# Top-p by a 27-step bit descent, and GAT weights factored into per-node exponentials, on one Trainium2 core

## The chip, the cores and the metric

The kernel runs on one core of a Trainium2 chip. The metric is the device time of one execution in microseconds (us); lower is better. A core has TensorE (PE, matrix products), VectorE (DVE), ScalarE (ACT, table functions and copies), GpSimd (POOL) and SyncE (SP, which issues most transfers).

## The reference

The input is `x`, 3327 nodes by 256 features, and `adj`, a dense 3327 x 3327 array with about 0.5% non-zero entries. Two graph layers follow one another, each added to its input, each behind a layer norm and a ReLU.

```
# layer 0, two steps
q = X @ W1.T @ W2.T;  k = X @ W3.T
probs = softmax(q @ k.T)                    # 3327 x 3327
idx = argsort(-probs);  sp = probs sorted;  cs = cumsum(sp)
keep_sorted = cs - sp < 0.9                 # top-p: largest entries up to 90% of the mass
A = probs * mask;  A = A / A.sum(-1)
Xf = R @ Xf;  Xa = A @ Xa                   # R: adj + identity, rows scaled to sum 1
Z += Xf @ U1[n].T + Xa @ U2[n].T

# layer 1, 4 heads of 64
hp = h @ W;  s = hp . a_src;  d = hp . a_dst          # per node and head
e = leaky_relu(s[i] + d[j], 0.2), -inf where adj[i, j] <= 0
out = elu(softmax(e) @ hp)
```

## The kernel before

Rows are cut into 26 tiles of 128 (`NT`), the last padded by one row. The program has two functions. `fast` computes everything and leaves a flag, `redo`; `general` is an older program for the same result, which runs only when the flag is set, behind a runtime branch in `tile_gnn`. The order of instructions on each engine is not written out by hand: a scheduler takes the operations in program order as their priority and lets later ones go ahead where earlier ones are not ready. [...]

**Layer 0.** `main`, `xf1` and `xa1` hold the features of all nodes with a column of ones. In each of the two steps, a first loop projects all tiles to `kt` (keys, transposed) and adds up a Gram matrix `gm`. Then 13 groups of two tiles follow. For a group:
- `exponentials` computes the queries, the logits against all keys in seven matrix products (L602), and their exponentials `e`, 128 x 3327 (L603). It also takes the mean and the variance of the logits from `gm`.
- `full_step` multiplies a tile of the adjacency with the features (L739) and scales the rows.
- `top_p` finds, for each row, the threshold under which the small entries sum to a tenth of the row. A guess comes from the moments of the logits by a polynomial (`QUANTILE`). `below` (L658) adds up the entries under a threshold in one pass of DVE over 3327 numbers. Three passes (first step) or four (second step) with secant updates bring the threshold near, a last pass and a search for maxima (L701 and on) pick the exact cut from a window of 32 values, and L728 sets the entries under it to zero.
- `attention_step` transposes `e` in blocks (L755), copies them out of PSUM (L757) and multiplies them with the features (L764).
- In the second step `add_up` applies `U1` and `U2` and prepares the layer norm.

The exponentials of the next group stand ahead of this group's `top_p` in the program. `epool` has four buffers for `e`, so two groups are in flight.

**Layer 1.** After the layer norm, each tile is projected to `hp` (four heads of 64 and a column of ones), and the scores `sd` are multiplied and reduced on DVE (L885, L886). The destination scores are spread over all partitions in `db`. A stage then reads the adjacency row by row (`an`), turns it into a mask of large negative numbers (L902), and takes for each row and head the largest masked score (L905). This gives the row maxima of the softmax, so that `pq` holds two terms per row: `s - top` and `0.2 s - top`.

The last loop goes over blocks of four row tiles, and in each over all 26 column tiles j. `broadcasts` spreads the row terms over partitions (`both`). Per j and head, the logit is the larger of two sums: ACT adds one (L954), DVE the other and takes the maximum (L955). Then DVE caps it at zero (L959), ACT takes the exponential (L960), DVE multiplies with the adjacency's sign (L963), and PE adds `hp` times the weights to one accumulator per head (L964). Column 65 of each accumulator holds the denominators. At the end of a block the accumulators are copied, transposed, divided, passed through ELU and stored.

Last, `redo` is made from marks in `met` that the top-p search left.

Of the kernel before, what the change touches and what calls it, by code (L numbers as in the profile page):

```python
# [24 lines left out]
H = 4  # L25
# [15 lines left out]

EVALS = (3, 4)
AIM = 13.0
WIN = 32
PIECES = 16
PIECE = 208
NC = 7
QUANTILE = (0.0080475, 0.1178442, 0.6505088, 2.0535298, 1.2031906)
# [416 lines left out]

@with_exitstack
def fast(
# [31 lines left out]
    met = const.tile([P, 5, STEPS * NT], F32, name="met")  # L499

# [12 lines left out]
    with ExitStack() as l0:  # L513
# [11 lines left out]
        gm = wpool.tile([DA, 2 * DA + 1], F32, name="gm")  # L525
        V.tensor_copy(gm[:, :DA], ident[:DA, :DA])
# [3 lines left out]
        scr = l0.enter_context(tc.tile_pool(name="scr", bufs=1))  # L530
# [41 lines left out]
        def exponentials(src, tiles):  # L572


            G = len(tiles)
            sm = small.tile([P, G], F32, name="sm")
            mu = small.tile([P, G], F32, name="mu")
            sq = small.tile([P, G], F32, name="sq")
            es = []
            for g, t in enumerate(tiles):  # L580
                ps = projected(w1, transposed(src, t))
                ut = small.tile([DA, P], F32, name="ut")
                S.copy(ut, ps)
                ps = ps_m.tile([DA, P], F32, name="pm")
                T.matmul(ps, w2, ut, start=True, stop=True)
                qt = small.tile([DA, P], F32, name="qt")
                S.copy(qt, ps)
                ps = ps_m.tile([P, 2 * DA + 1], F32, name="pm")
                T.matmul(ps, qt, gm, start=True, stop=True)
                qg = small.tile([P, 2 * DA + 1], F32, name="qg")  # L590
                S.copy(qg, ps)
                V.tensor_copy(mu[:, g : g + 1], qg[:, 2 * DA :])
                V.scalar_tensor_tensor(
                    qg[:, :DA], qg[:, :DA], 1.0, qg[:, DA : 2 * DA], ALU.mult, ALU.mult, accum_out=sq[:, g : g + 1]
                )
                e = epool.tile([P, NP], F32, name="e")
                nc.gpsimd.memset(e[:, N:], 0.0)
                parts = small.tile([P, NC], F32, name="parts")
                for c in range(NC):
                    w = min(512, N - 512 * c)  # L600
                    pl = ps_l.tile([P, 512], F32, name="pl")
                    T.matmul(pl[:, :w], qt, kt[:, 512 * c : 512 * c + w], start=True, stop=True)  # L602
                    S.activation(  # L603
                        e[:, 512 * c : 512 * c + w], pl[:, :w], AF.Exp, accum_out=parts[:, c : c + 1]
                    )
                V.tensor_reduce(sm[:, g : g + 1], parts, AX.X, ALU.add)
                es.append(e)
            return es, sm, mu, sq

        def top_p(es, sm, mu, sq, n, tiles):  # L610
# [3 lines left out]

            G, i0 = len(es), n * NT + tiles[0]

            def small_tile(name):
                return small.tile([P, G], F32, name=name)

            b = small_tile("b")  # L620
            V.tensor_scalar(b, sm, 1.0 - TOP_P, None, ALU.mult)
            V.tensor_copy(met[:, 0, i0 : i0 + G], sm)
            var = small_tile("var")
            V.tensor_mul(var, mu, mu)
            V.tensor_sub(var, sq, var)
            V.tensor_scalar(var, var, 1e-6, None, ALU.max)
            sg = small_tile("sg")
            S.activation(sg, var, AF.Ln)
            S.activation(sg, sg, AF.Exp, scale=0.5)
            u = small_tile("u")  # L630
            S.activation(u, b, AF.Ln, scale=1.0 / N)
            V.tensor_sub(u, u, mu)
            V.scalar_tensor_tensor(u, var, -0.5, u, ALU.mult, ALU.add)
            V.tensor_scalar(u, u, -6.0, -0.3, ALU.max, ALU.min)
            w = small_tile("w")
            V.tensor_scalar(w, u, QUANTILE[0], None, ALU.mult)
            for c in QUANTILE[1:-1]:
                V.scalar_tensor_tensor(w, w, c, u, ALU.add, ALU.mult)
            V.scalar_tensor_tensor(w, w, QUANTILE[-1], sg, ALU.add, ALU.add)
            t = small_tile("t0")  # L640
            V.tensor_mul(t, w, sg)
            V.tensor_add(t, t, mu)
            S.activation(t, t, AF.Exp)
            g = small_tile("g0")
            V.tensor_mul(g, w, w)
            S.activation(g, g, AF.Exp, scale=0.5)
            V.scalar_tensor_tensor(g, g, math.sqrt(2 * math.pi) / N, sg, ALU.mult, ALU.mult)
            V.tensor_scalar(g, g, 0.25, None, ALU.min)

            k2 = small_tile("k2")  # L650
            V.scalar_tensor_tensor(k2, t, 225.0, t, ALU.mult, ALU.mult)

            def below(th, outs=None, dst=None):
                sums = small_tile("sums") if dst is None else dst
                ys = []
                for k, e in enumerate(es):
                    y = scr.tile([P, N], F32, name="y", bufs=1)
                    V.scalar_tensor_tensor(  # L658
                        y, e[:, :N], th[:, k : k + 1], e[:, :N], ALU.is_lt, ALU.mult, accum_out=sums[:, k : k + 1]
                    )  # L660
                    if outs is not None:
                        outs(k, y)
                return sums

            tp = bp = None
            for k in range(EVALS[n]):
                B = below(t)
                if k > 0:
                    dt, dB, kg = small_tile("dt"), small_tile("dB"), small_tile("kg")
                    V.tensor_sub(dt, t, tp)  # L670
                    V.tensor_sub(dB, B, bp)
                    V.tensor_mul(dt, dt, dB)
                    V.tensor_mul(dB, dB, dB)
                    V.tensor_add(dB, dB, k2)
                    V.tensor_mul(kg, k2, g)
                    V.tensor_add(dt, dt, kg)
                    V.reciprocal(dB, dB)
                    V.tensor_mul(g, dt, dB)
                x, d, nt = small_tile("x"), small_tile("d"), small_tile("nt")
                V.tensor_scalar(x, g, AIM / 2, 1.0, ALU.mult, ALU.add)  # L680
                V.reciprocal(x, x)
                V.scalar_tensor_tensor(x, x, AIM, t, ALU.mult, ALU.mult)
                V.tensor_sub(d, b, B)
                V.tensor_add(d, d, x)
                V.tensor_mul(d, d, g)
                V.tensor_add(d, d, t)
                V.scalar_tensor_tensor(d, t, 0.25, d, ALU.mult, ALU.max)
                V.scalar_tensor_tensor(nt, t, 8.0, d, ALU.mult, ALU.min)
                tp, bp, t = t, B, nt

            up = small_tile("up")
            V.tensor_sub(up, sm, b)
            V.scalar_tensor_tensor(up, t, 16.0, up, ALU.mult, ALU.is_ge)
            V.scalar_tensor_tensor(up, up, BIG, t, ALU.mult, ALU.max)

            cands = small.tile([P, G, PIECES, 8], F32, name="cands")
            wins = small.tile([P, G, WIN], F32, name="wins")

            def window(k, y):
                for c in range(PIECES):  # L700
                    V.max(cands[:, k, c, :], y[:, c * PIECE : min(c * PIECE + PIECE, N)])  # L701

            B = below(up, window)
            V.tensor_reduce(met[:, 1, i0 : i0 + G], cands[:, :, :, 7], AX.X, ALU.max)
            room = small_tile("room")
            V.tensor_sub(room, B, b)
            for k, e in enumerate(es):
                flat = cands[:, k].rearrange("p c r -> p (c r)")
                for r in range(WIN // 8):
                    top = wins[:, k, 8 * r : 8 * r + 8]  # L710
                    V.max(top, flat)
                    if r < WIN // 8 - 1:
                        V.match_replace(flat, top, flat, -1.0)
                win = wins[:, k, :]
                cum = small.tile([P, WIN], F32, name="cum")
                V.tensor_tensor_scan(cum, win, win, 0.0, ALU.add, ALU.bypass)
                keep = small.tile([P, WIN], F32, name="keep")
                V.scalar_tensor_tensor(
                    keep, cum, room[:, k : k + 1], win, ALU.subtract, ALU.is_lt,
                    accum_out=met[:, 2, i0 + k : i0 + k + 1],  # L720
# [339 lines left out]
```

## Time and profile before

| | |
|---|---|
| median of 3 runs | 4061.26 us (4054.56 to 4062.52) |
| profiled execution | 4062.52 us, span 4060.7 us |
| mean granted TensorE clock | 0.855 of full |
| layer 0, from the span's start to the last `top_p` | 0 to 2308 us |
| last attention and sums of layer 0 | 2308 to 2362 us |
| layer norm and projection of layer 1 | 2362 to 2480 us |
| row maxima (L902, L905) | 2480 to 2930 us |
| loop over blocks, and the end | 2930 to 4061 us |

Times in the profile are from the first instruction of the span. A row of a group gives the source line, the engine, the operation, the tiles that it writes and reads with their sizes, the number of instructions, the busy time in us, the mean of one in ns, and then the engine's idle time just before such instructions with what ended it. PEclk is the granted clock of TensorE in tenths, in 40 equal slices of the span. In the timeline the columns are start and duration in us, engine, line, operation and tiles; start to start is the pitch, and durations of neighbours overlap a little.

### The profile page before, as it was taken

Reading aid. Unit: us, or ns where it says so; the run is one execution under the profiler, and the core shown is the slowest. Engines: PE = TensorE matmul, PEld = TensorE weight load, DVE = VectorE, ACT = ScalarE, POOL = GpSimd, SP = SyncE. Lnnn points to the kernel's source line nnn. Section 1 sums busy time; section 2 is a strip of 40 time slices with the busy share of each in tenths; the row PEclk is TensorE's granted clock in tenths of the full one; section 3 lists DMA queues with packets and bytes.
Section 4 is the critical chain, followed back from the end, with each engine's and each line's share of the span. In section 5 each row is a group of like instructions: output and inputs, shape, how many; then the busy total and the mean of one; then the engine's idle time right before and its main releaser. Section 6 shows DMA issues by size and latency. Waiting matters only on the chain.

```text
span 4060.7 us, 34714 instructions
## 1 busy us (share of the span) xinstructions
PE 2928.3 (72%) x11286; PEld 1822.5 (45%) x11286; DVE 3364.6 (83%) x7077; ACT 1616.4 (40%) x2997; POOL 56.7 (1%) x167
## 2 busy tenths in 40 slices
PE   6689999999994999999999942000076667666665
PEld 4366676676861776677766831000022122121122
DVE  2498788788607998788887779999499999999998
ACT  3423333333232333323333222000177777777765
POOL 0000000000000000000000020000000000000000
PEclk9589999899995999999999966555589899998888
DMA  3011111111210111111111121232111111111110
GB/s 99 0 34 34 51 51 34 47 55 34 68 34 0 37 38 38 39 60 45 38 38 37 54 75 67 102 116 101 37 42 42 45 44 44 44 47 42 47 34 25
DMA packets 80959, 195.13 MB, mean 48 GB/s; under 512 B 5890, under 2 KB 64001, under 8 KB 77441
## 3 DMA queue, kind: packets, MB, share of 16 engines
q1 hardware_dynamic: 78384, 190.83, 14.6%
q10 hardware_dynamic: 2384, 1.98, 0.2%
q8 instruction: 91, 1.49, 0.2%
q14 instruction: 100, 0.82, 0.1%
HBM read 189.39 MB, written 3.41 MB: 47 GB/s over the span
## 4 chain that ended last, share of the span: by engine, by line
DVE 61%; PE 26%; ACT 6%; issue 4%; another core or an unknown queue 1%; DMA 1%; POOL 1%; ACTq 0%; DVEq 0%; POOLq 0%; SPq 0%
DVE y L658 16%; DVE e L955 10%; DVE junk L905 9%; PE pl L602 8%; DVE e L963 8%; PE acc L739 6%; DVE e L959 4%; DVE cands L701 4%; PE acc L764 2%; PE pm L789 1%; PE pm L569 1%; DVE an L902 1%; PE acc L964 1%; ACT e L603 1%
## 5 line engine op out<-in xcount | busy, mean ns | idle before, releaser
L964 PE MATMUL acc<-e,hp 128*65 128x512 f32 (+1 forms) x1456 | 721.5, 644 | 344.1 <-DVE e L963 344.1
L964 PEld LDWEIGHTS acc<-e,hp 128*65 128x65 f32 x1456 | 209.0, 155 | 831.4 <-DVE e L963 587.6
L757 ACT COPY et<-pt 128x512 f32<-128x512 f32 (+1 forms) x364 | 199.5, 555 | 747.2 <-PE pt L755 747.2
L658 DVE SCALAR_TENSOR_TENSOR y<-e,nt 128x3327 f32<-128x3327 f32 x130 | 478.8, 3683 | 2.3
L955 DVE SCALAR_TENSOR_TENSOR e<-both,sd,e 128x512 f32<-128x512 f32 (+1 forms) x728 | 472.4, 712 | 8.7 <-ACT e L954 8.7
L954 ACT ACTIVATE e<-both,dlow 128x512 f32<-128x512 f32 (+1 forms) x728 | 443.8, 678 | 52.6 <-PE acc L964 52.6
L602 PE MATMUL pl<-kt,qt 64*128 64x512 f32 (+1 forms) x728 | 411.4, 705 | 53.5 <-ACT e L603 53.5
L963 DVE SCALAR_TENSOR_TENSOR e<-adjb,e 128x512 f32<-128x512 f32 (+1 forms) x728 | 428.2, 652 | 4.4 <-ACT e L960 4.2
L960 ACT ACTIVATE e<-e 128x2048 f32<-128x2048 f32 (+1 forms) x182 | 325.3, 1787 | 244.3 <-DVE e L959 244.2
L905 DVE CUSTOM_DVE_ANT_0 junk<-an,db 128x3327 bf16<-128x3327 f32 (+1 forms) x104 | 370.7, 3624 | 2.0 <-ACT db L890 1.2
L935 PE MATMUL pb<-ident,pq 128*128 128x128 f32 x208 | 32.1, 301 | 469.6 <-DVE pq L914 466.3
L739 PE MATMUL acc<-main,at 128*128 128x257 f32 x1352 | 336.6, 402 | 0.8 <-DMA at<-in_adjt_dram 0.8
L739 PE MATMUL acc<-xf,at 128*128 128x257 f32 x1352 | 336.5, 398 | 0.3 <-ACT xa L768 0.3
L764 PE MATMUL acc<-xa,et 128*128 128x257 f32 x1352 | 322.3, 382 | 3.8 <-ACT et L757 3.8
L764 PE MATMUL acc<-main,et 128*128 128x257 f32 x1352 | 324.3, 384 | 0.2
L739 PEld LDWEIGHTS acc<-main,at 128*128 128x128 f32 x1352 | 263.3, 201 | 52.4 <-issue 13.1
L739 PEld LDWEIGHTS acc<-xf,at 128*128 128x128 f32 x1352 | 257.5, 198 | 49.1 <-issue 14.0
L602 PEld LDWEIGHTS pl<-kt,qt 64*128 64x128 f32 x728 | 146.3, 225 | 292.7 <-ACT e L603 227.9
L755 PE MATMUL pt<-ident,e 128*128 128x128 f32 x1352 | 202.2, 275 | 94.0 <-DVE e L728 94.0
L603 ACT ACTIVATE e<-pl 128x512 f32<-128x512 f32 (+1 forms) x364 | 205.2, 564 | 158.4 <-PE pl L602 155.4
L764 PEld LDWEIGHTS acc<-main,et 128*128 128x128 f32 x1352 | 246.0, 191 | 35.3 <-ACT et L757 6.2
L764 PEld LDWEIGHTS acc<-xa,et 128*128 128x128 f32 x1352 | 245.4, 191 | 36.4 <-ACT et L757 7.6
(192 smaller groups left out, 3359.0 us busy)
## 6 DMA issues: line engine op xcount, KB each, us to landing
at<-in_adjt_dram SPq DMA_DIRECT2D x104, 832.0 KB, 4.5
an<-in_adj_dram SPq DMA_DIRECT2D x25, 1663.5 KB, 6.9
adjb<-in_adjt_dram SPq DMA_DIRECT2D x78, 512.0 KB, 3.8
main<-in_x_dram SPq DMA_DIRECT2D x26, 128.0 KB, 3.2
xh<-in_x_dram SPq DMA_DIRECT2D x26, 128.0 KB, 2.0
xr<-in_x_dram SPq DMA_DIRECT2D x26, 128.0 KB, 2.0
adjb<-in_adjt_dram SPq DMA_DIRECT2D x13, 256.0 KB, 2.8
out_dram<-r SPq DMA_DIRECT2D x25, 128.0 KB, 1.8
```

The source lines that it names most:

```text
L602: T.matmul(pl[:, :w], qt, kt[:, 512 * c : 512 * c + w], start=True, stop=True)
L603: S.activation(e[:, 512 * c : 512 * c + w], pl[:, :w], AF.Exp, accum_out=parts[:, c : c + 1])
L658: V.scalar_tensor_tensor(y, e[:, :N], th[:, k : k + 1], e[:, :N], ALU.is_lt, ALU.mult, accum_out=sums[:, k : k + 1])
L739: T.matmul(acc, at[:, j - j0, :], src[:, j, :], start=(j == 0), stop=(j == NT - 1))
L755: T.transpose(pt[:, k, :], e[:, (j0 + k) * P : (j0 + k + 1) * P], ident)
L764: T.matmul(acc, et[:, j - j0, :], src[:, j, :], start=(j == 0), stop=(j == NT - 1))
L905: V.tensor_tensor_reduce(junk[:p], an[:p], db[:p, k, :N], scale=1.0, scalar=-BIG, op0=ALU.add, op1=ALU.max, accum_out=top[:p, t, k : k + 1],)
L954: S.activation(e[:, k, :w], both[:, 1, k, :w], AF.Identity, bias=dlow[:, j, k : k + 1])
L955: V.scalar_tensor_tensor(e[:, k, :w], both[:, 0, k, :w], sd[:, j, 1, k : k + 1], e[:, k, :w], ALU.add, ALU.max)
L960: S.activation(e[:, :, :w], e[:, :, :w], AF.Exp)
L963: V.scalar_tensor_tensor(ek, adjb[:, :n, j % JC, :], 0.0, ek, ALU.is_gt, ALU.mult)
L964: T.matmul(acc[k][:, :w], hp[:, j, k, :], e[:, k, :w], start=(j == 0), stop=(j == NT - 1))
```

## The change

The diff changes `fast` in three places.

1. Layer 0's `top_p` is replaced by the one that `general` has. The logits are copied out of PSUM, DVE takes each row's maximum, and one exponential per tile makes `e`. The threshold is then found bit by bit: 27 times a candidate is formed by setting one bit of the cut, all entries at or above it are added up, and the bit is kept where the sum reaches 90% of the row. Ties at the cut are ranked by a running sum. The Gram matrix, the moments, the window and `met` go.
2. In layer 1, the weight of j for i is written as exp(d[j]) times the larger of exp(0.8 s[i]) and exp(-0.8 d[j]), up to a factor of the row that the division removes. `hp` and its last column are scaled by exp(d); `both` holds exp(0.8 s) and `low` holds exp(-0.8 d). Per head and j one DVE operation takes the maximum and multiplies with a bf16 mask, which is made once for all four heads. The row maxima and their reading of the adjacency go. The scores come out of the projection, by eight more columns in its weights.
3. `redo` is set when a score exceeds 40 in size (`REACH`).

Cut to its core:

```diff
 def exponentials(src, tiles):
-    ps = ps_m.tile([P, 2 * DA + 1], F32, name="pm")
-    T.matmul(ps, qt, gm, start=True, stop=True)
...
-    S.activation(e[:, 512 * c : 512 * c + w], pl[:, :w], AF.Exp, accum_out=parts[:, c : c + 1])
+    S.copy(e[:, c : c + w], pl[:, :w])
+    V.tensor_reduce(mx, e[:, :N], AX.X, ALU.max)
+    V.tensor_scalar(nb, mx, -1.0, SHIFT, ALU.mult, ALU.add)
+    S.activation(e[:, :N], e[:, :N], AF.Exp, bias=nb, accum_out=st[:, g : g + 1])
+    V.tensor_scalar(th, st, TOP_P, None, ALU.mult)
-def top_p(es, sm, mu, sq, n, tiles):
...
+def top_p(es, th):
+    V.memset(cut, LOWEST)
+    for b in range(BITS - 1, -1, -1):
+        V.tensor_scalar(cand.bitcast(I32), cut.bitcast(I32), 1 << b, None, ALU.bitwise_or)
+        for g, e in enumerate(es):
+            junk = scr.tile([P, N], BF16, name="scr")
+            V.scalar_tensor_tensor(junk, e[:, :N], cand[:, g : g + 1], e[:, :N], ALU.is_ge, ALU.mult,
+                                   accum_out=sums[:, g : g + 1])
+        V.tensor_tensor(ok, sums, th, ALU.is_ge)
+        V.copy_predicated(cut, ok, cand)
+    V.reciprocal(rcut, cut)
+    for g, e in enumerate(es):
+        V.tensor_scalar(ties, e[:, :N], c, None, ALU.is_equal)
+        V.scalar_tensor_tensor(e[:, :N], e[:, :N], c, e[:, :N], ALU.is_gt, ALU.mult, accum_out=above)
+        V.tensor_tensor_scan(rank, ties, ties, 0.0, ALU.add, ALU.max)
+        V.tensor_sub(room, th[:, g : g + 1], above)
+        V.tensor_scalar(room, room, rcut[:, g : g + 1], 1.0, ALU.mult, ALU.add)
+        V.scalar_tensor_tensor(ties, rank, room, ties, ALU.is_lt, ALU.mult)
+        V.scalar_tensor_tensor(e[:, :N], ties, c, e[:, :N], ALU.mult, ALU.add)
...
-    S.copy(hp[:, t, :, :FH], pm)
-    for k in range(2):
-        V.tensor_mul(prod, hp[:, t, :, :FH], a_all[:, :, k * FH : (k + 1) * FH])
-        V.tensor_reduce(sd[:, t, k, :], prod, AX.X, ALU.add)
...
+    V.tensor_copy(sd[:, :, t, :], pm[:, H * FH :].rearrange("p (k h) -> p k h", k=2))
+    S.activation(hp[:, t, :, FH], sd[:, 1, t, :], AF.Exp)
+    V.tensor_mul(hp[:, t, :, :FH], pm[:, : H * FH]..., hp[:, t, :, FH : FH + 1].to_broadcast([P, H, FH]))
+S.activation(low, sd[:, 1], AF.Exp, scale=ALPHA - 1.0)
-for t in range(NT):
-    nc.sync.dma_start(an[:p], adj[t * P : t * P + p, :])
-    V.tensor_scalar(an[:p], an[:p], 0.0, -BIG, ALU.is_le, ALU.mult)
-    for k in range(H):
-        V.tensor_tensor_reduce(junk[:p], an[:p], db[:p, k, :N], ..., accum_out=top[:p, t, k : k + 1])
...
+    mask = mpool.tile([P, JC, K * P], BF16, name="mask")
+    for a in range(JC):
+        V.tensor_scalar(mask[:, a, :w]..., adjb[:, :n, a, :], 0.0, None, ALU.is_gt)
     for k in range(H):
-        S.activation(e[:, k, :w], both[:, 1, k, :w], AF.Identity, bias=dlow[:, j, k : k + 1])
-        V.scalar_tensor_tensor(e[:, k, :w], both[:, 0, k, :w], sd[:, j, 1, k : k + 1], e[:, k, :w], ALU.add, ALU.max)
-    V.tensor_scalar(e[:, :, :w], e[:, :, :w], 0.0, None, ALU.min)
-    S.activation(e[:, :, :w], e[:, :, :w], AF.Exp)
-    for k in range(H):
-        V.scalar_tensor_tensor(ek, adjb[:, :n, j % JC, :], 0.0, ek, ALU.is_gt, ALU.mult)
+        V.scalar_tensor_tensor(e[:, k, :w], both[:, k, :w], low[:, j, k : k + 1], mask[:, j % JC, :w],
+                               ALU.max, ALU.mult)
         T.matmul(acc[k][:, :w], hp[:, j, k, :], e[:, k, :w], start=(j == 0), stop=(j == NT - 1))
...
+V.tensor_scalar(bad, bad, REACH, 0.0, ALU.is_le, ALU.is_equal)
```

## The prediction, made before the change was run

> **What bounds the kernel now.** I read the page's busy shares first, then the chain that ended last, then the groups by form, then two pieces of the timeline.
>
> ```profile
> PE 2928.3 (72%) x11286; PEld 1822.5 (45%) x11286; DVE 3364.6 (83%) x7077; ACT 1616.4 (40%) x2997; POOL 56.7 (1%) x167
> PEclk9589999899995999999999966555589899998888
> DVE 61%; PE 26%; ACT 6%; issue 4%; another core or an unknown queue 1%; DMA 1%; POOL 1%; ACTq 0%; DVEq 0%; POOLq 0%; SPq 0%
> ```
>
> DVE carries the kernel; PE is second. The average hides three stages. In layer 0 (0 to 2308 us of the span) both engines are nearly full: from 1272 to 2308 us, PE 90% and DVE 88% busy. From 2480 to 2930 us DVE works alone (the row maxima of L905), and waits 49.6 us for the last adjacency rows. From 2930 to 4061 us DVE is 97% busy.
>
> ```profile
> L658 DVE SCALAR_TENSOR_TENSOR y<-e,nt 128x3327 f32<-128x3327 f32 x130 | 478.8, 3683 | 2.3
> L955 DVE SCALAR_TENSOR_TENSOR e<-both,sd,e 128x512 f32<-128x512 f32 x624 | 428.1, 751 | 8.7 <-ACT e L954 8.7
> L963 DVE SCALAR_TENSOR_TENSOR e<-adjb,e 128x512 f32<-128x512 f32 x624 | 391.1, 691 | 1.6 <-ACT e L960 1.5
> L905 DVE CUSTOM_DVE_ANT_0 junk<-an,db 128x3327 bf16<-128x3327 f32 x100 | 356.4, 3623 | 2.0 <-ACT db L890 1.2
> L902 DVE TENSOR_SCALAR an<-an 128x3327 f32<-128x3327 f32 x25 | 47.2, 1889 | 5.1 <-DMA an<-in_adj_dram 5.1
> L716 DVE TENSOR_TENSOR_SCAN cum<-wins 128x32 f32<-128x32 f32 x52 | 10.3, 213 | 0.0
> ```
>
> These are the prices: a threshold pass over 3327 numbers takes 3.68 us. Today there are 234 of them (130+52+52). One group of two tiles, from the timeline:
>
> ```profile
> 888.08 3.68 DVE L658 SCALAR_TENSOR_TENSOR y<-e,nt 128x3327 f32<-128x3327 f32 x1
> ...
> 891.81 3.68 DVE L658 SCALAR_TENSOR_TENSOR y<-e,nt 128x3327 f32<-128x3327 f32 x1
> 895.42 0.08 DVE L658 DVE_READ_ACCUMULATOR y<-e,nt 128x1 f32 x1
> 895.54 0.16 DVE L671 TENSOR_TENSOR dB<-sums 128x2 f32<-128x2 f32 x1
> ...
> 895.73 0.16 DVE L672 TENSOR_TENSOR dt<-dt,dB 128x2 f32<-128x2 f32 x1
> ...
> 895.93 0.16 DVE L673 TENSOR_TENSOR dB<-dB 128x2 f32<-128x2 f32 x1
> ```
>
> Two passes and the sum's read take 7.46 us (888.08 to 895.54); each further small operation that needs the one before costs 0.20 us.
>
> [...] 3327 elements in 1.89 us (L902) against 3.68 us (L658). [...] 213 ns for 32 elements against 183 ns for the plain two-source L722 of that size. [...] 0.50 while PE idles, 1.00 in 1130 to 1200 us; but L602, on 64 partitions, stays at 0.50 while PE is busy (110 to 180 us).
>
> **The change, part by part.** It does two opposite things.
>
> *Layer 0 (top-p) gets a fixed 27-step bit descent* in place of the guess, 3 or 4 secant passes and a window. Per group of two tiles on DVE:
> - 27 steps, each two passes up to the dependent operation (7.46), then compare, predicated copy and the next candidate (3 x 0.20): 8.05 us, so 217.4. The int operation and the predicated copy are not in the trace; I price them as other 2-element operations, at 0.14 to 0.3 each (-4 to +5 us per group).
> - Ending, per tile: equality to bf16 1.85 (L902's start-to-start[...]); keep-above pass 3.73; scan of 3327 elements 7.1[...]; two small operations, of which 0.2 shows; rank pass 3.6[...]; final pass 3.6. That is 20.1, two tiles 40.2, with the reciprocal 40.4.
> - Row maximum 3.55 per tile[...], with its small operations 7.7 per group.
> - The diffusion step's epilogue and attention's reciprocals 1.5; in step 1, add_up's layer-norm work 2.3 more.
>
> Sum 267.0 (step 0) and 269.3 (step 1), against a period of about 76 and 85 us now. Thirteen groups each: 3471 + 3501 = 6972.
>
> Beside this lie PE (1974 us busy from 140 to 2308 us now, less the Gram and moment matmuls; some 75 us per group) and ACT (copies in place of exponentials, then one 3.0 us exponential per tile, from L960's 1.91 us for 2048). Both fit under 267 us with two groups of e in flight (epool has four buffers). The bf16 scratch with two buffers is written and read by DVE alone: no wait. The DMAs of at stay and get three times the time. Removing 4 table loads per group costs or gains nothing; DVE covers them.
>
> **A wait that may be added:** [...] within top_p of group i+1 stand the reciprocals of group i's attention and the row maxima of group i+2. Each blocks every pass behind it when PE is late. Now DVE loses 8 us per group so (81.7 us for L606 in ten groups of step 1), under a full PE. Afterwards PE is mostly idle but starts cold, and L602 runs at half clock: 11 us per tile instead of 6. I take 4 us per group, 104 us; bounds 0 and 20 (520).
>
> Edges: 140 us to the first pass as now (the Gram matmuls saved, row maximum and long exponential gained). Between the steps, last attention 15, kt 3, exponentials, maximum and exponential of two tiles 34: 52 us, 140 now (1098 to 1238), when PE still owes diffusion steps. After the last top_p, attention and add_up of one tile: 25.
>
> *Layer 1.* Layer norm unchanged, 51. Projection: a_src and a_dst are folded into w, so per tile DVE has layer norm, 8-element copy and one scaled evacuation (1.0 us), PE four transposes of 0.11 and four 264-column records of 0.22 (1.3 us): PE bounds, 26 x 1.3 plus latency = 40, 50 now. The row-maximum stage goes: all of 2480 to 2930, its 26 adj loads on SP's queue and their 49.6 us wait with it.
>
> The loop per j: DVE drops from L955, L959, L963 (start to start 0.66 x 4, 1.14, 0.60 x 4: 6.19 us per j) to four max-and-mask operations with a per-partition scalar, 0.66 each as L955, and half of a mask pair, 0.34[...]: 3.0. ACT has nothing left in it. PE: eight records of 512 columns at 0.427 us (timeline at full clock) = 3.41 us, so **PE becomes the bound here**. 156 full rounds 533, 26 half rounds 44, 104 broadcast transposes 11, output transposes 8: 596. DVE under it: 156 x 3.0 + 26 x 1.8 + 39 for outputs = 554. Four accumulators free one by one 1.9 us before they are reused, so block ends cost little; 19 for cold starts and ends: 615 (590 to 700), against 1115 now. First loads and masks 10; the end, whose two tiny verdict steps wait for output DMAs as now, 18.
>
> Total: 140 + 3471 + 52 + 3501 + 25 + 51 + 40 + 10 + 615 + 18 + 104 = 8027. Outside the span lie 1.8 us (4062.52 against 4060.7). The profiled run is 1.3 us above the median of 4061.26, which is nothing here. **Forecast 8030.** Layer 0 goes from 2362 to 7293 us (stalls included), layer 1 from 1700 to 734.
>
> **Rivals.**
> - *DVE held by PE's order:* 10 to 20 us per group instead of 4 gives 8190 to 8450. For it: today's 8 us. Against: PE has 190 us to spare per group. Wholly serial (attention, exponentials and diffusion never beside top_p, some 80 us per group): 10,000. Against that, the timeline at 895.9 to 925 us shows attention of one group under another's passes.
> - *Cheaper ending:* [...] 7760 to 7940.
> - *The old program runs as well:* the verdict asks whether any source or destination score exceeds 40. Evaluated on the reference's inputs the largest are 2.27 and 1.98, so the branch is not taken. If taken, about 17,000 (another 7293 for layer 0, and 1700 for a layer 1 like the present one).
> - *Faster after all:* [...] The rest is 8030 - 1404 x 3.67 = 2877, so a pass must fall below 0.84 us, a quarter of its price, before the total passes 4061. L905 with bf16 output speaks against it. A half-price pass gives 5450, still slower. At 0.7 us it would be 3860.
> - *The change is not what it says:* if the secant stayed and only layer 1 changed, some 3100. The diff removes it outright.
>
> **Chances.** Forecast case (7950 to 8150) 0.57; DVE held 0.22, of it wholly serial 0.02; cheaper ending 0.19; branch 0.01; faster 0.01. The range 7780 to 8420 leaves about a fifth out. Faster 0.01, same (within 0.2%, about what a measurement of this kernel can tell) 0.005, slower 0.985.
>
> **What would show it.** Right: 1404 threshold passes near 3.68 us; DVE above 93% in layer 0 with PE near 30%; no row-maximum stage; in the last 640 us PE above 90% and DVE just below it; scan rows near 7.1 us. Wrong: passes near 1.8 us, DVE waits for PE or ACT beyond 10 us per group, masks near 0.7 us with DVE bounding the loop, or a second program behind the first.

## The result, and the profile after

The changed kernel takes **7782.96 us** (median of 4 runs, 7776.36 to 7788.15) against 4061.89 us before: 1.9165 times as long, 95% interval 1.9132 to 1.9198. The profiled execution took 7778.63 us, its span is 7776.8 us. The forecast was 8030 us, in a range from 7780 to 8420; the result lies 247 us under the forecast and 3 us inside the range's lower edge.

The page of the changed kernel answers line by line to the one before: busy shares, clock, chain.

```profile
PE 2681.8 (34%) x10662; PEld 1762.1 (23%) x10662; DVE 7401.8 (95%) x7093; ACT 785.1 (10%) x1440; POOL 53.8 (1%) x115
PEclk7566656665666567557657756775676577657999
DVE 78%; PE 18%; issue 2%; ACT 1%; DMA 0%; POOL 0%; ACTq 0%; DVEq 0%; POOLq 0%; SPq 0%
```

DVE went from 3365 to 7402 us. PE's work hardly changed, but it is spread over twice the time: its busy share fell from 72% to 34%, and its mean clock from 0.855 to 0.669. In layer 0 that could cost little, since from 140 to 7028 us DVE is 97.5% busy and PE 28%. The last four slices, which hold layer 1, show a clock of 7, 9, 9, 9 tenths.

The groups by form, as before with the tiles of the new lines:

```profile
L601 DVE SCALAR_TENSOR_TENSOR scr<-e,cand 128x3327 bf16<-128x3327 f32 x1404 | 5124.3, 3684 | 32.1 <-ACT e L582 9.3
L830 DVE SCALAR_TENSOR_TENSOR e<-both,low,mask 128x512 f32<-128x512 f32 x624 | 426.6, 747 | 35.6 <-PE acc L833 35.6
L619 DVE TENSOR_TENSOR_SCAN scr<-scr 128x3327 uint16<-128x3327 bf16 x52 | 368.5, 7086 | 0.0
L623 DVE SCALAR_TENSOR_TENSOR scr<-scr,room 128x3327 bf16<-128x3327 uint16 x52 | 191.7, 3687 | 1.8
L579 DVE TENSOR_REDUCE mx<-e 128x1 f32<-128x3327 f32 x52 | 187.9, 3613 | 53.9 <-ACT e L577 53.9
L613 DVE TENSOR_SCALAR scr<-e,cut 128x3327 bf16<-128x3327 f32 x52 | 101.0, 1942 | 0.0
L823 DVE TENSOR_SCALAR mask<-adjb 128x512 bf16<-128x512 f32 x156 | 59.2, 422 | 4.4 <-DMA adjb<-in_adjt_dram 2.6
```

One row holds two thirds of the time: 1404 passes, 5124 us. A pass with bf16 scratch costs 3684 ns, as the fp32 one did (3683). The scan costs 7086 ns, nearly twice a pass. The rank pass L623 has two-byte inputs and output throughout and still takes 3687. The row maxima of layer 1 and the three operations per head and j are gone.

One bit step, from the timeline (start, duration):

```profile
3023.73 3.69 DVE L601 SCALAR_TENSOR_TENSOR scr<-e,cand 128x3327 bf16<-128x3327 f32 x1
3027.34 0.08 DVE L601 DVE_READ_ACCUMULATOR scr<-e,cand 128x1 f32 x1
3027.34 3.68 DVE L601 SCALAR_TENSOR_TENSOR scr<-e,cand 128x3327 bf16<-128x3327 f32 x1
3030.94 0.08 DVE L601 DVE_READ_ACCUMULATOR scr<-e,cand 128x1 f32 x1
3031.06 0.16 DVE L606 TENSOR_TENSOR ok<-sums,th 128x2 int32<-128x2 f32 x1
3031.26 0.16 DVE L607 COPY_PREDICATED cut<-ok,cand 128x2 f32<-128x2 int32 x1
3031.46 0.17 DVE L597 TENSOR_SCALAR cand<-cut 128x2 int32<-128x2 int32 x1
3031.66 3.69 DVE L601 SCALAR_TENSOR_TENSOR scr<-e,cand 128x3327 bf16<-128x3327 f32 x1
```

From step to step 7.93 us (3023.73 to 3031.66), with the three small operations 0.20 us apart.

Last, two stretches of layer 1's new loop. The columns are the stretch and its length, then busy us and instruction counts of PE, PEld, DVE, ACT and POOL, the clock, the DMA share and GB/s.

```profile
7200.00:7400.00 200.00, 200.00 (x516) 67.69 (x515) 185.41 (x322) 12.43 (x24) 6.62 (x8) 1.00 0.30 86
7400.00:7600.00 200.00, 200.00 (x519) 67.96 (x518) 182.92 (x316) 12.33 (x24) 6.61 (x8) 1.00 0.28 81
```

PE is full at full clock, DVE at 92%, ACT at 6%. The loop, from the first to the last product (L833), takes 596.7 us, of which PE is busy for 595; before it took 1093 (L964).

### The profile page after: what moved, and what is told of

It reads as the page before. It is cut to its first block, busy times and chain, and to the rows that moved or that the text cites. A ratio compares the mean times of both kernels' runs of the same rounds, so it can differ in the third digit from the quotient of the medians.

```text
span 7776.8 us, 31642 instructions
## 1 busy us (share of the span) xinstructions
PE 2681.8 (34%) x10662; PEld 1762.1 (23%) x10662; DVE 7401.8 (95%) x7093; ACT 785.1 (10%) x1440; POOL 53.8 (1%) x115
## 4 chain that ended last, share of the span: by engine, by line
DVE 78%; PE 18%; issue 2%; ACT 1%; DMA 0%; POOL 0%; ACTq 0%; DVEq 0%; POOLq 0%; SPq 0%
DVE scr L601 58%; PE acc L833 7%; DVE scr L619 5%; PE acc L660 3%; PE pl L576 3%; DVE scr L623 2%; DVE e L615 2%; DVE e L624 2%; DVE mx L579 2%; DVE cand L597 1%; PE pm L685 1%; DVE cut L607 1%; DVE ok L606 1%; DVE scr L613 1%; PE acc L635 1%
## 5 line engine op out<-in xcount | busy, mean ns | idle before, releaser
L601 DVE SCALAR_TENSOR_TENSOR scr<-e,cand 128x3327 bf16<-128x3327 f32 x1404 | 5124.3, 3684 | 32.1 <-ACT e L582 9.3
L651 PEld LDWEIGHTS pt<-ident,e 128*128 128x128 f32 x1352 | 189.0, 158 | 4943.7 <-DVE e L624 4677.2
L833 PE MATMUL acc<-e,hp 128*65 128x512 f32 (+1 forms) x1456 | 585.6, 562 | 1.8 <-DVE e L830 1.8
L830 DVE SCALAR_TENSOR_TENSOR e<-both,low,mask 128x512 f32<-128x512 f32 (+1 forms) x728 | 469.2, 709 | 38.8 <-PE acc L833 38.8
L619 DVE TENSOR_TENSOR_SCAN scr<-scr 128x3327 uint16<-128x3327 bf16 x52 | 368.5, 7086 | 0.0
L833 PEld LDWEIGHTS acc<-e,hp 128*65 128x65 f32 x1456 | 198.1, 138 | 368.3 <-issue 255.5
L579 DVE TENSOR_REDUCE mx<-e 128x1 f32<-128x3327 f32 x52 | 187.9, 3613 | 53.9 <-ACT e L577 53.9
L577 ACT COPY e<-pl 128x512 f32<-128x512 f32 (+1 forms) x364 | 196.6, 555 | 163.8 <-PE pl L576 163.6
L615 DVE SCALAR_TENSOR_TENSOR e<-e,cut 128x3327 f32<-128x3327 f32 x52 | 191.6, 3684 | 5.9 <-DVE scr L613 0.9
L623 DVE SCALAR_TENSOR_TENSOR scr<-scr,room 128x3327 bf16<-128x3327 uint16 x52 | 191.7, 3687 | 1.8
L624 DVE SCALAR_TENSOR_TENSOR e<-scr,cut,e 128x3327 f32<-128x3327 bf16 x52 | 191.5, 3684 | 1.9
```

What stands on the lines that cost most here:

```text
L579: V.tensor_reduce(mx, e[:, :N], AX.X, ALU.max)
L601: V.scalar_tensor_tensor(junk, e[:, :N], cand[:, g : g + 1], e[:, :N], ALU.is_ge, ALU.mult, accum_out=sums[:, g : g + 1],)
L615: V.scalar_tensor_tensor(e[:, :N], e[:, :N], c, e[:, :N], ALU.is_gt, ALU.mult, accum_out=above)
L619: V.tensor_tensor_scan(rank, ties, ties, 0.0, ALU.add, ALU.max)
L623: V.scalar_tensor_tensor(ties, rank, room, ties, ALU.is_lt, ALU.mult)
L624: V.scalar_tensor_tensor(e[:, :N], ties, c, e[:, :N], ALU.mult, ALU.add)
```

## Experiments

The theory: the two halves are separate stages. Layer 0 costs the number of passes times their price, since DVE has cover for everything else; layer 1 gains a whole stage and a loop that PE now bounds. The rivals: the halves act on each other; PE's order holds DVE; DVE still bounds the new loop. Times below are medians.

**One half each.** The two files are joined where `gat` is allocated. In e1_layer1_only `redo` takes the marks of the top-p search and that of `REACH`.

```diff
# e1_layer1_only: layer 0 of before
+        V.tensor_tensor(one[:, 0:1], reach[:, 0:1], reach[:, 1:2], ALU.max)
+        V.tensor_scalar(one[:, 0:1], one[:, 0:1], REACH, 0.0, ALU.is_le, ALU.is_equal)
+        V.tensor_tensor(bad[:, 0:1], bad[:, 0:1], one[:, 0:1], ALU.max)
# e2_layer0_only: layer 1 of before
+        V.tensor_reduce(reach, sd.rearrange("p t k h -> p k t h"), AX.XY, ALU.max, apply_absolute_value=True)
```

> Layer 0 of the kernel before with layer 1 of the change; the verdict joins both marks. Theory (the two halves are separate stages, each bounded by its own DVE or PE work): layer 0 ends as before at about 2362 us, layer 1 takes the 718 us that it took in the changed kernel, so 3080 us plus or minus 20. Rival (the halves interact, for instance layer 1 is short in the changed kernel only because transfers and clock are relieved after a light layer 0): above 3150.

> Layer 0 of the change with layer 1 of the kernel before. Theory of separate stages: layer 0 ends at about 7059 us as in the changed kernel, and layer 1 adds the 1700 us of before: 8760 plus or minus 30. Rival of interaction: off by more than 60.

Measured: 3077.88 us for layer 1 alone (0.7595 of before, 0.7576 to 0.7614) and 8763.69 us for layer 0 alone (2.161, 2.1564 to 2.1655). Their sum is 11841.6; before (4059.72 beside them) and after give 11842.7. The halves add up to 1 us, well within the intervals (some 8 and 18 us), so an interaction of more than some 20 us is excluded. Layer 0's change costs 4704 us (8763.69 - 4059.72), layer 1's saves 982. Layer 1's loop takes 596.8 us in e1_layer1_only too.

**Fewer steps.**

```diff
-            for b in range(BITS - 1, -1, -1):
+            for b in range(BITS - 1, BITS - 14, -1):
```

> The changed kernel with the first 14 of the 27 bit steps; the lowest 13 bits of the cut stay zero, so the threshold is coarser. Theory (each step costs two passes and three dependent operations, 7.93 us per group, and nothing else hides or limits it): 13 x 26 x 7.93 = 2680 less, 5100 plus or minus 40. Rival (PE or ACT limits part of a group): less is saved, above 5250.

The expectation miscounted its own edit: the range stops before bit 13, so 13 steps run and 14 are removed. By the same rule that is 14 x 26 x 7.93 = 2887 less, 4896. Measured 4905.82 us, 2877 less, or 7.90 us per step and group. With only half of the passes per group PE and ACT still fit beside them, so they limit nothing that shows.

**The row maxima alone.**

```diff
-        top = wpool.tile([P, NT, H], F32, name="top")      # with db, an, L902, L905
...
+        V.tensor_copy(pq[:, :, 0, :], s_all)
+        V.tensor_scalar(pq[:, :, 1, :], s_all, ALPHA, None, ALU.mult)
-                V.tensor_scalar(e[:, :, :w], e[:, :, :w], 0.0, None, ALU.min)
+                V.tensor_scalar(e[:, :, :w], e[:, :, :w], 60.0, None, ALU.min)
```

> The kernel before without the row-maximum stage of layer 1: the row terms are s and 0.2 s as they are, and the cap at zero becomes a cap at 60, at the same cost. Theory: the stage lay on the path whole, so 450 us plus the spread of destination scores (some 10 us) go: 3600 plus or minus 20, and the loop stays at 1115. Rival (part of the stage was hidden beside the projection, or the loop's first loads were): 3650 or more.

Measured: 3607.08 us (0.888, 0.8852 to 0.8909), 453 less. The loop stays at 1095 us from first to last product. So layer 1's 982 us are 453 for the stage, some 498 for the loop (1095 to 597), and some 30 for the rest.

**What bounds the new loop.** On e1_layer1_only, the weights are made bf16, or each mask is made twice, or both.

```diff
# e5_bf16_weights
-    hp = gat.tile([P, NT, H, FH + 1], F32, name="hp")
+    hp = gat.tile([P, NT, H, FH + 1], BF16, name="hp")
-                e = tpool.tile([P, H, K * P], F32, name="e")
+                e = tpool.tile([P, H, K * P], BF16, name="e")
# e7_masks_twice on e1_layer1_only, e8_bf16_masks_twice on e5_bf16_weights
-                    for a in range(JC):
+                    for a in [*range(JC), *range(JC)]:
```

> e1_layer1_only with the attention weights e and the scaled features hp in bf16[...]. Theory (PE bounds the new loop at 8 fp32 records per j; DVE is just under it, 183 of 200 us busy): [...] DVE becomes the bound, so the loop goes from 597 to 546 to 565 us and the whole from 3078 to about 3035 (3020 to 3055). Rival (DVE bounds the loop already, or the start and the ends of blocks do): within 10 us of 3078. Second rival (bf16 output puts the max-and-mask operation in a faster mode): below 2950.

> e1_layer1_only with each mask made twice: 182 more mask operations on DVE, 58 us at their start to start. Theory (PE bound, DVE with 50 us of slack in the loop): 0 to 20 us more, up to 3098. Rival (DVE bound): 58 us more, 3136.

> e5_bf16_weights with each mask made twice. Theory (there DVE bounds the loop): the whole 58 us over e5_bf16_weights, plus or minus 10. Rival (PE or block ends still bound): under 30 us over it.

| | median us | ratio to before (95%) | loop us |
|---|---|---|---|
| e1_layer1_only | 3077.88 | 0.7595 (0.7576 to 0.7614) | 596.8 |
| e7_masks_twice | 3091.06 | 0.7612 (0.7597 to 0.7626) | 607.7 |
| e5_bf16_weights | 3037.08 | 0.7477 (0.7464 to 0.7489) | 550.5 |
| e8_bf16_masks_twice | 3091.05 | 0.7614 (0.7602 to 0.7626) | 606.7 |

The second masks are 58 us of DVE work, estimated from their number and start to start. The same work cost 13 us where PE bounds the loop and 54 where DVE does (the loop alone, in one execution of each: 11 and 56). The 13 us are hardly clear of noise, since the two intervals overlap; that they are far fewer than 54 is clear. With double masks the two kernels meet, since both then run at DVE's pace. The windows of e5_bf16_weights and of e7_masks_twice say it directly, in this order:

```profile
2500.00:2700.00 200.00, 152.09 (x315) 41.22 (x314) 197.28 (x345) 11.71 (x24) 6.63 (x8) 0.53 0.30 87
```

```profile
2500.00:2700.00 200.00, 196.04 (x498) 65.67 (x497) 199.19 (x377) 12.33 (x24) 6.61 (x8) 0.99 0.28 82
```

In both DVE is full. The max-and-mask operation of e5_bf16_weights kept its price with bf16 output (747 ns with fp32), so the second rival falls:

```profile
L946 DVE SCALAR_TENSOR_TENSOR e<-both,low,mask 128x512 bf16<-128x512 f32 x624 | 422.4, 746 | 0.4
```

**The cover of layer 0.** The changed kernel with three and with two buffers for `e`.

```diff
-        epool = l0.enter_context(tc.tile_pool(name="epool", bufs=4))
+        epool = l0.enter_context(tc.tile_pool(name="epool", bufs=3))   # e9_two_e: bufs=2
```

> The changed kernel with three buffers for e in place of four, so that the second tile of the next group cannot be made beside this group's top-p. Theory (the changed layer 0 is DVE alone only because two groups are in flight; without that cover the attention of one tile, the logits, the row maximum and the exponential of the next stand before the passes): 8 to 30 us more per group, so 7990 to 8550. Rival (PE has so much room that the order of the buffers does not matter): within 60 us of 7783.

> The changed kernel with two buffers for e, one group in flight. Theory (with three buffers the second tile's 20 us ending on DVE still covered the first tile's attention and the next tile's logits, so only the 3.6 us exponential showed; with two, the attention of the second tile, the logits of the last new tile, its maximum and its exponential have no passes beside them): 15 to 30 us more per group than 7783, so 8150 to 8550. Rival (the scheduler finds cover here too): under 7950.

Three buffers: 7857.92 us (1.9354, 1.9324 to 1.9383), 75 more. That is neither case as it was put. DVE's waits (who waited, for whom, us in total, times, longest) name the place, in the changed kernel and with three buffers:

```profile
DVE mx L579 <- ACT e L577: 53.9, 22, 15.5
DVE th L585 <- ACT e L582: 16.7, 3, 9.5
DVE scr L601 <- ACT e L582: 9.3, 2, 5.5
```

```profile
DVE th L585 <- ACT e L582: 96.2, 26, 9.5
```

What grew is the wait for the second tile's exponential, now in every group and 3.7 us on average; the other changes nearly cancel. I had overlooked that this group's second tile has its 20 us ending on DVE while PE turns the first tile and makes the next logits (in the trace of e6_three_e from 2221 to 2242 us). Two buffers take that cover away too: 8257.72 us (2.0336, 2.0292 to 2.0379), 475 more, as expected. Its waits:

```profile
DVE mx L579 <- ACT e L577: 340.2, 28, 20.4
DVE th L585 <- ACT e L582: 97.5, 26, 10.3
DVE scr L601 <- ACT e L582: 95.6, 26, 9.0
```

Against the changed kernel these three grew by 453 us. So two groups in flight are worth 475 us here, and with four buffers the waits for PE and ACT are few.

**The ending.**

```diff
-            rcut = small.tile([P, G], F32, name="rcut")      # with ties, rank, room and their passes
...
+                V.scalar_tensor_tensor(e[:, :N], e[:, :N], c, e[:, :N], ALU.is_ge, ALU.mult)
```

> The changed kernel without the ranking of ties: equality, scan, rank and final pass go, and one pass keeps all entries at or above the cut. Theory (the ending stands on DVE's path whole, from the starts in the trace 2.04 + 7.01 + 0.42 + 3.72 + 3.60 per tile): 52 x 16.8 = 873 less, 6910 plus or minus 25. Rival (the ending covers PE's attention of the first tile, so that part of what is removed comes back as a wait): above 7000.

Measured: 6903.82 us (1.7003, 1.6966 to 1.704), 879 less, where 873 were expected. The whole of what was removed was on the path, the scan with it.

**A version faster than both.** e1_layer1_only is that already. Since DVE bounds e5_bf16_weights, its largest row was split into a maximum and a product:

```diff
-        both = rows.tile([P, H, K * P], F32, name="both")
+        both = rows.tile([P, H, K * P], BF16, name="both")
-                    V.scalar_tensor_tensor(e[:, k, :w], both[:, k, :w], low[:, j, k : k + 1], mask[:, j % JC, :w],
-                                           ALU.max, ALU.mult)
+                    V.tensor_scalar(e[:, k, :w], both[:, k, :w], low[:, j, k : k + 1], None, ALU.max)
+                V.tensor_mul(e[:, :, :w], e[:, :, :w], mask[:, j % JC, :w].unsqueeze(1).to_broadcast([P, H, w]))
```

> e5_bf16_weights with both in bf16 and the max-and-mask split into operations[...]: per head a one-source maximum with the per-partition scalar, then one product of all four heads with the mask. Theory[...]: 1.95 us in place of 2.65 per j, about 110 less than e5_bf16_weights, 2925 plus or minus 25. Rival[...]: 3100 or more.

Measured: **2948.24 us** (0.7269, 0.725 to 0.7288), 89 under e5_bf16_weights and 27% under the kernel before. Its groups by form:

```profile
L947 DVE TENSOR_TENSOR e<-e,mask 128x2048 bf16<-128x2048 bf16 x156 | 189.4, 1214 | 0.0
L946 DVE TENSOR_SCALAR e<-both,low 128x512 bf16<-128x512 bf16 x624 | 178.4, 344 | 1.3 <-ACT both L923 1.3
```

The product takes 1.14 us start to start in the timeline for the four heads' 2048 elements, with the mask read again for each head; before the split four operations took 0.66 each. The 1.95 us per j of the expectation leave 0.20 for each maximum, which no run had shown; the timeline has 0.26. Over 624 of them that is 37 us more than estimated, and the loop, down from 550.5 to 473 us, gave 78 in place of 110. The other 11 us of the 89 lie outside the loop, where the single traces of e1_layer1_only and e7_masks_twice, alike up to there, differ by 10 (the loop starts at 2450.7 and 2460.3 us).

## Why the prediction was right, and by how much it missed

The signs, the mechanism and nearly all prices held: 1404 passes at 3.68 us, DVE at 97.5% and PE at 28% in layer 0, no row-maximum stage, PE at 96% and DVE at 89% in the last 640 us, scans at 7.09 us. That the range held the result was luck. The median lies 3 us above its lower edge, and two of the four executions lie under it. The forecast case itself (7950 to 8150) missed, and the cheaper ending (scan or rank pass under its price in the sum), the one case under it, did not happen: the scan is 7.09 us (7.1 in the sum) and the rank pass 3.69. The sum was too high by many small terms of one sign. The 250 us of the profiled execution (8028.8 to 7778.6) are, as far as they were traced, in these terms, all read from one execution:

- *The 27 steps:* 8.05 us forecast, 7.93 measured; 27 x 26 x 0.12 = 84. The price of two passes was taken from before at 888.08 to 895.54, and there a small operation stands between the two and delays the second by 0.12 us (its line stands below the list). The bit descent has none: 3.61 us from pass to pass, 3.73 before. The integer operation and the predicated copy, which no trace had shown, cost 169 and 162 ns, as guessed.
- *DVE held by PE's order:* 4 us per group forecast. The idle times of the trace inside the groups (L579, L663) are 0 to 2.5 us in step 0 and 0 to 1.8 in step 1, about 1.2 on average: some 74 less. The rival that made this larger was far off; even with three buffers only 75 us were added.
- *Other DVE work of a group:* some 1.3 us per group less, 34, although the ending of a tile takes 20.4 us where the sum has 20.1. Part of that is a misreading: L902 follows at 1.92 us start to start in the trace, not at 1.85, and the equality at 2.04.
- *Row maxima counted in all 26 groups:* the last group of each step has no next one to prepare (258 us in place of 262.5 and 265.9), and the first ones already lie in the start; 15.
- *The start:* the first group ends its steps at 340.6 us, 357.4 forecast, 17 less, since DVE takes up the first tile's pass (at 96.1 us) while the second is being made. Some 3 us of this stand in the first term too.
- *Edges and layer 1:* the gap between the steps 46 (52 forecast), the last attention 31 (25), layer norm 53 (51), projection 39 (40), first loads 8 (10), loop 597 (615), end 21 (18): 16 less in sum.

That is 240 of 250; the rest was not traced.

```profile
891.69 0.15 DVE L670 TENSOR_TENSOR dt<-nt,t 128x2 f32<-128x2 f32 x1
```

The loop deserves a word: PE's sum of 596 us was met (595 busy of 596.7), and the 19 us added for cold starts (such as that of layer 1's projection in the kernel before, where PE is busy at a clock of 0.50 from 2415 to 2420 us and at 0.95 in the next 5) and for block ends were not needed: the clock is 1.00 and PE is idle for under 2 us in the whole loop. That accumulators come free in turn, as the prediction argued, fits this and was not tested alone.

The rival on the other side, cheaper passes with bf16 scratch, is refuted by the row of L601 itself: 3684 ns. The old program did not run: no second program stands behind the first in the span.

The prices by form, each for 3327 elements: a one-source operation on fp32 took 1889 ns with fp32 output (L902 before) and 1942 with bf16 output (L613), the reduction of the row maximum 3613 (L579), the two-source operation with a scalar 3684 with bf16 output (L601) and 3683 with fp32 (L658 before). The scan takes 7086 against 3687 of the rank pass beside it, close to twice. The 7.1 us for it in the sum had no scan of this length behind it; the trace of before shows only 213 ns for a scan of 32 elements (L716) against 183 for a two-source operation of that size (L722). Why it takes twice as long was not tested.

## What to carry to other kernels

A fixed-count search on a bound engine is priced by multiplication: count the full-length passes, take the pass from the trace, and look for a reason why it should not add up; here 1404 x 3.65 us are two thirds of the time, while a gain of 982 us elsewhere in the same diff, 24% of the time before, was invisible in the total. Split such a change and measure the halves: one of them alone was 0.7595 of the time before. Where two engines are both nearly full, as PE and DVE in the new loop (100% and 92%), adding work to one of them shows which bounds it: 13 us against 54 for the same work.

## What the runs showed that was not expected

In the bf16 loop of e5_bf16_weights PE shows 152 of 200 us busy and yet a clock of 0.53; its products of 512 columns take 577 ns on average. The fp32 loop, full at 100%, has 1.00, and e7_masks_twice, at 98%, 0.99. e11_packed_weights, with only 124 of 200 us busy and longer gaps, has 0.67. In the kernel before it is 0.50 both from 2480 to 2930 us, where PE is idle, and from 110 to 180 us, where PE is busy for 61.8 of 70. So the busy share alone does not tell the clock. In the trace of e11_packed_weights bf16 products come in bursts of four and follow each other at 0.21 us in some bursts and at 0.43 in others. Such a burst of the fast kind, and the two us around it, where the clock (the third figure from the end) is 1.00:

```profile
2502.34 1.02 PE L951 MATMUL acc<-e,hp 128*65 128x512 bf16 x4 [1.01 <-DVE e L947]
2502.00:2504.00 2.00, 1.02 (x4) 0.44 (x4) 2.00 (x6) 0.00 (x0) 0.00 (x0) 1.00 0.51 181
```

In the changed kernel an fp32 product of 512 columns is two records at 0.43 us each, at a clock of 1.00, so a bf16 product at 0.21 takes a quarter of that. In e5_bf16_weights the products follow at 0.66 us, the pace of DVE's max-and-mask operations, and PE's busy time fell only from 200 to 152 of 200 us; the time came out as forecast because DVE bounds that loop. What keeps the clock low there was not tested.

A bf16 maximum with a per-partition fp32 scalar takes 344 ns for 512 elements and 278 for 256: the second 256 elements add only 66 ns, so most of the time is a fixed part (some 212 ns, an estimate from the two: 278 - 66), and the operation gained less than was estimated (0.26 us start to start in place of 0.20).
